# Router logits and the shared expert's first layer as one 264-column product with the tokens as weights

## The chip, the cores and the metric

The kernel runs on one core of one Trainium2 chip. The metric is device time in microseconds (us): the median of three runs, and, where a trace is read, the time of one profiled execution. All arithmetic on tensors is in float32, except for a few 0/1 matrices in bfloat16 in the routing.

## The reference, cut to what matters

The input is x of 2 sequences by 4096 positions by 512 features. A first part (test-time training) runs through the positions in order and keeps a state W for each sequence. A second part is a mixture of experts. Each is added to its input and layer-normalized.

```
x = layernorm(x + ttt(x))                  # W changes with every position
shared = silu(X @ sW1 + sb1) @ sW2 + sb2   # sW1: 512 x 256, sW2: 256 x 512
logits = X @ routing_W.T + expert_bias     # 8 experts: 8 columns
activation = sqrt(softplus(logits)); the 2 largest of 8 are kept as weights
routed = sum over the kept experts of weight * (silu(X @ rW1 + rb1) @ rW2 + rb2)
out = layernorm(x + shared + routed)
```

## The kernel before, in words

**Chunks and steps.** The positions are cut into 32 chunks of 128. A chunk holds 128 positions of both sequences, so 256 tokens (B = 2, T = 256). A loop over c = 0 to 31 makes one step for each chunk. In step c the following generators are interleaved.

- `step(c)` is the recurrence. It makes the residual R (matmuls `pr`), the output `po`, a triangular solve by three products (`pz` on TensorE, `Z` on VectorE), transposes of K (`pk`, copied to SBUF as the tile `K`), the solved product `pe` with `F` behind it, and the update of the state (`pw` on TensorE, `W` on VectorE, four times per sequence, and `pb` with `brep`).
- `prep(c + 1)` makes K and Q of the next chunk (`pkq`, copied by ScalarE) and their inner products (`pa`).
- `invert(c)` inverts small triangular blocks on VectorE (`X`), turns them through HBM (`dX`, `CT`) and makes `D` and `DT`, with which `pn` begins.
- `shared(c - 1)` is the mixture's first half for the chunk before. It finishes the normalization, transposes the tokens (`pt`, copied by ScalarE as `yT`), starts the routing (`router`: logits `pl` and `lg`, then `u`, Exp, `w`, Ln, ranks, `chosen`, Sqrt), computes the shared expert (`ph` and Silu into `h`, then `py`), and places the tokens by expert (`pq`, `place`, `row`, and scattered writes into tables in HBM).
- In steps 24 to 27 the routed expert tiles of chunks 0 to 22 run as well (`pg`, `phe`, `he`, `pye`). At the end of step 23, and again in step 31, `plan` turns the tables into lists of gathers (`codes`, `pc`, `gidx`). In steps 28 to 31 part of the results is collected (`acc` on VectorE). The rest follows behind step 31, with the routed tiles of chunks 23 to 30 and all experts for chunk 31.

**What sets the order.** `interleave` runs the generators so that each advances in proportion to a total given with it; the numbers after `yield` are the shares done. Chunk c's `shared` has the total SHARED = 15 (with 10 more for `plan`, and doubled in step 31). For TensorE and VectorE the order in which instructions are made this way is kept; each engine works through its own in order. ScalarE's order is the scheduler's.

**Buffers.** PSUM has three pools: `ps_p` with two buffers (`pkq`, `pa`, `pn`, `pz`), `ps_s` with three (`pr`, `po`, `pk`, `pe`, `pw`, `pb`) and `ps_f` with three (`pt`, `pl`, `ph`, `pq`, `py` and the routed tiles). The two `po` of a step keep two of `ps_s` until late, so that `pk`, `pe` and `pw` follow each other through the rest.

**Around the change.** The logits of a chunk are eight matmuls (2 sequences by 4 slices of 128 features) with a slice of `yT` as weights and 8 columns of `rw` moving through (line 480). The shared expert's first layer is eight matmuls with a 128 x 128 block of `w1` as weights and the 256 tokens moving through (line 594); its output has hidden units on the partitions, which is what `py` needs. Silu follows from PSUM with the bias per partition (line 597). The transposed K is copied from PSUM by ScalarE (line 439).

Of the kernel before, what the change touches and what calls it, by code (L numbers as in the profile page):

```python
# [40 lines left out]
F32 = mybir.dt.float32  # L41
# [3 lines left out]
ALU = mybir.AluOpType  # L45
AX = mybir.AxisListType

P = 128
# [53 lines left out]
def postln_block(ctx: ExitStack, tc: tile.TileContext, x, xT, thK, thV, thQ, w0, b0, masks, blk,  # L102
                 unit, order, rw, eb, w1s, b1s, w2s, b2s, b2e, wcat, out):
    nc = tc.nc
    B, S, D = x.shape
    NCH = S // P
    DC = D // P
    E = rw.shape[1]
    HF = w1s.shape[1]
    HC = HF // P  # L110
    T = B * P
# [6 lines left out]
    const = ctx.enter_context(tc.tile_pool(name="const", bufs=1))  # L118
# [6 lines left out]
    hp = ctx.enter_context(tc.tile_pool(name="hp", bufs=1))  # L125
# [3 lines left out]
    sm = ctx.enter_context(tc.tile_pool(name="sm", bufs=2))  # L129
# [4 lines left out]
    ps_f = ctx.enter_context(tc.tile_pool(name="ps_f", bufs=3, space=PSUM))  # L134
# [42 lines left out]
    load_x(0)  # L177
    load_x(1)

    rw_sb = const.tile([P, DC, E], F32, tag="rw", name="rw")  # L180
    nc.sync.dma_start(out=rw_sb, in_=rw.rearrange("(c p) e -> p c e", p=P))
    eb_sb = const.tile([P, E], F32, tag="eb", name="eb")
    nc.sync.dma_start(out=eb_sb, in_=eb.partition_broadcast(P))
    b1_sb = const.tile([P, HC], F32, tag="b1", name="b1")
# [2 lines left out]
    nc.sync.dma_start(out=b2_sb, in_=b2s.partition_broadcast(P))  # L187
    b1e_sb = const.tile([P, E, HC], F32, tag="b1e", name="b1e")
    nc.sync.dma_start(out=b1e_sb, in_=wcat[:, OB1:OB2].rearrange("(e p) h -> p e h", p=P))
    w1_sb = const.tile([P, DC, HF], F32, tag="w1", name="w1")  # L190
    nc.sync.dma_start(out=w1_sb, in_=w1s.rearrange("(c p) h -> p c h", p=P))
    w2_sb = const.tile([P, HC, D], F32, tag="w2", name="w2")
    nc.sync.dma_start(out=w2_sb, in_=w2s.rearrange("(c p) d -> p c d", p=P))

# [197 lines left out]
    def step(c):  # L392
# [25 lines left out]
        for s in range(B):  # L418

            ps = ps_s.tile([P, D], F32, tag="ps", name=f"po_{c}_{s}")  # L420
            for ec in range(DC):
                nc.tensor.matmul(ps, KQ[:, ec, s, 1, :], W[s][:, ec, :],  # L422
                                 start=(ec == 0), stop=False)
                if ec == 1:
                    if s == 0:
                        next(levels)
                    yield 2.0
            O.append(ps)
            if s == 0:
                next(levels)  # L430
            yield 2.0
            if s == 0:

                for r in range(B):
                    ps = ps_s.tile([P, DC, P], F32, tag="ps", name=f"pk_{c}_{r}")
                    for ec in range(DC):
                        nc.tensor.transpose(ps[:, ec, :], KQ[:, ec, r, 0, :], ident)
                    k = stepp.tile([P, DC, P], F32, tag="K", name=f"K_{c}_{r}")
                    nc.scalar.copy(k, ps)
                    K.append(k)  # L440
                    if r == 0:
                        Y = next(levels)
                    yield 1.5
# [26 lines left out]
        normed[c] = y, norm[1]  # L470


    def router(c, yT):
        def small(tag, shape=(P, B, E), bufs=1):
            return sm.tile(list(shape), F32, tag=tag, name=f"{tag}_{c}", bufs=bufs)

        ps = ps_f.tile([P, B, E], F32, tag="pf", name=f"pl_{c}")
        for s in range(B):
            for dc in range(DC):
                nc.tensor.matmul(ps[:, s, :], yT[:, dc, s, :], rw_sb[:, dc, :],  # L480
                                 start=(dc == 0), stop=(dc == DC - 1))
        lg = small("lg")
        nc.vector.tensor_tensor(lg, ps, eb_sb[:, None, :].broadcast_to([P, B, E]), ALU.add)


        u = small("u")
# [76 lines left out]
    def shared(c):  # L563

        gr = of_step.get(c)
        if gr and c == gr.c0:
            gr.begin()
        y, norm = normed.pop(c)
        next(norm)
        yield 1.5  # L570
        yT = ytp.tile([P, DC, B, P], F32, tag="yT", name=f"yT_{c}")
        for dc in range(0, DC, 2):
            ps = ps_f.tile([P, 2, B, P], F32, tag="pf", name=f"pt_{c}_{dc}")
            for s in range(B):
# [11 lines left out]
        yield 1.5  # L586
        for s in range(B):
            nc.gpsimd.tensor_tensor(y[:, s, :], y[:, s, :], b2_sb, ALU.add)
        ps = ps_f.tile([P, HC, T], F32, tag="pf", name=f"ph_{c}")
        h = hp.tile([P, HC, B, P], F32, tag="h", name=f"h_{c}")  # L590
        for hc in range(HC):
            cf = next(routing)
            for dc in range(DC):
                nc.tensor.matmul(ps[:, hc, :], w1_sb[:, dc, hc * P:(hc + 1) * P],
                                 yT[:, dc].rearrange("p s t -> p (s t)"),
                                 start=(dc == 0), stop=(dc == DC - 1))
            nc.scalar.activation(h[:, hc].rearrange("p s t -> p (s t)"), ps[:, hc, :],
                                 AF.Silu, bias=b1_sb[:, hc:hc + 1])
            yield 2.0
        next(routing, None)  # L600
        yield 1.0
        next(routing, None)
        if not gr:

            ps = ps_f.tile([E, B, P], F32, tag="pf", name=f"pct_{c}")
            for s in range(B):
                nc.tensor.transpose(ps[:, s, :], cf[:, s, :], ident)
            cfT = stepp.tile([E, B, P], F32, tag="K", name=f"cfT_{c}")
            nc.scalar.copy(cfT, ps)
            b2e_sb = stepp.tile([E, D], F32, tag="K", name="b2e")  # L610
            nc.sync.dma_start(out=b2e_sb, in_=b2e)
            yield 1.0
        for s in range(B):
            ps = ps_f.tile([P, D], F32, tag="pf", name=f"py_{c}_{s}")
            for hc in range(HC):
                nc.tensor.matmul(ps, h[:, hc, s, :], w2_sb[:, hc, :], start=(hc == 0),
                                 stop=(hc == HC - 1 and gr is not None))
            if not gr:
                nc.tensor.matmul(ps, cfT[:, s, :], b2e_sb, start=False, stop=True)
            nc.vector.tensor_tensor(y[:, s, :], ps, y[:, s, :], ALU.add)  # L620
            yield 2.0
        if not gr:
            last.extend((y, yT, cf))
            return
        nc.sync.dma_start(out=gr.base[rows].rearrange("(s p) d -> p s d", p=P), in_=y)
        if c == gr.c0 + gr.n - 1:
            yield from plan(gr)
# [350 lines left out]
```

## Time and the profile before

| What | Value |
|---|---|
| Time, median of three runs (lowest, highest) | 2758.53 us (2753.56, 2760.92) |
| Profiled execution: time, span of the trace | 2757.97 us, 2756.0 us |
| Busy share of the span: TensorE, VectorE, ScalarE, GpSimd | 96%, 47%, 27%, 28% |
| Granted TensorE clock, mean over the span | 0.989 |
| `ph`, line 594: instructions, mean of one | 512, 379 ns |
| `pl`, line 480: instructions, mean of one | 512, 251 ns |
| Transposes `pk`, line 437: instructions, mean of one | 256, 273 ns |
| Copy of K on ScalarE, line 439: instructions, mean of one | 64, 580 ns |

TensorE's instructions overlap, so the mean duration of one is longer than the time it takes from the engine. What it takes is read from the timeline, as the distance from one start to the next. A float32 matmul is recorded as two instructions, a float32 transpose as one; so 512 instructions of `pl` are 256 matmuls, eight for each of the 32 chunks. PEld is the loading of weights, which runs beside the matmuls. A line like "A <- B" in the waits says that an instruction writing A waited for one writing B.

### The profile page before, as it was taken

How to read it: one execution, taken by the hardware profiler on the slowest of the kernel's cores; microseconds unless marked ns; L12 is line 12 of the kernel's file. 1: busy time of each engine (PE TensorE's matmuls, PEld its weight loads, DVE VectorE, ACT ScalarE, POOL GpSimd, SP SyncE). 2: the span in 40 equal slices, each digit the busy share in tenths (PEclk: the TensorE clock that was granted, in tenths of full speed). 3: DMA queues.
4: the chain of work that ended last, by engine and by line, in shares of the span. 5: the costliest groups of instructions: out<-in, count | busy, mean ns of one | idle time of the engine just before them, and what ended most of it. 6: DMA issues, size and time to landing. Idle time of an engine off the chain costs nothing. (4 is left out here: it accounts for less than half of the span.)

```text
span 2756.0 us, 32318 instructions
## 1 busy us (share of the span) xinstructions
PE 2658.1 (96%) x10977; PEld 1718.3 (62%) x10977; DVE 1292.1 (47%) x4093; ACT 755.7 (27%) x1474; POOL 766.5 (28%) x767
## 2 busy tenths in 40 slices
PE   8999999999999999999999999999999999889887
PEld 6666666666666666666666676767667655546664
DVE  2455555444445555544445413223132388773238
ACT  1211122222221122222222322323223133334447
POOL 0121111111111111111112433243342355454445
PEclk9999999999999999999999999999999999999998
DMA  4122212111111211121112534344333467775666
GB/s 161 36 50 61 63 40 41 48 40 40 40 40 42 54 48 48 41 48 40 40 40 56 169 71 126 121 107 135 89 126 101 102 180 197 206 223 197 204 213 225
DMA packets 148787, 269.42 MB, mean 98 GB/s; under 512 B 61180, under 2 KB 62940, under 8 KB 145040
## 3 DMA queue, kind: packets, MB, share of 16 engines
q1 hardware_dynamic: 90608, 139.50, 17.5%
q0 software_dynamic: 49584, 111.61, 14.7%
q10 hardware_dynamic: 8432, 16.25, 1.7%
q8 instruction: 88, 1.44, 0.2%
q14 instruction: 75, 0.61, 0.1%
HBM read 333.37 MB, written 88.64 MB: 153 GB/s over the span
## 5 line engine op out<-in xcount | busy, mean ns | idle before, releaser
L347 DVE SCALAR_TENSOR_TENSOR X<-L,X 128x31 f32<-128x31 f32 (+22 forms) x1472 | 332.7, 274 | 27.5 <-DMA L<-dL 10.5
L557 POOL DMA_INDIRECT gt<-code,ri x124 | 123.7, 998 | 710.7 <-DVE ri L554 682.0
L790 PEld LDWEIGHTS phe<-gT,wb 128*128 128x128 f32 x2208 | 270.7, 194 | 75.4 <-issue 68.9
L804 DVE TENSOR_TENSOR o<-pye,wb 128x512 f32<-128x512 f32 x138 | 95.4, 691 | 452.1 <-PE pye L801 436.6
L790 PE MATMUL phe<-gT,wb 128*128 128x128 f32 x2208 | 273.7, 278 | 16.2 <-DMA wb<-wcat_in,widx 15.5
L801 PE MATMUL pye<-wb,he 128*128 128x512 f32 x552 | 266.8, 605 | 21.1 <-ACT he L794 20.4
L457 PE MATMUL pw<-F,K 128*128 128x512 f32 x512 | 244.6, 608 | 9.6 <-DVE W L458 8.1
L304 PE MATMUL pkq<-xT,thK 128*128 128x256 f32 x1024 | 242.9, 381 | 7.6 <-DMA thK<-thK_in 7.6
L304 PEld LDWEIGHTS pkq<-xT,thK 128*128 128x128 f32 x1024 | 195.3, 191 | 82.2 <-issue 61.6
L304 PE MATMUL pkq<-xT,thQ 128*128 128x256 f32 x1024 | 241.9, 380 | 2.6 <-ACT N L378 2.6
L422 PE MATMUL po<-W,kq 128*128 128x512 f32 x512 | 244.2, 600 | 0.0
L402 PE MATMUL pr<-thV,xT 128*128 128x512 f32 x512 | 241.8, 604 | 0.0
L407 PE MATMUL pr<-W,kq 128*128 128x512 f32 x512 | 240.1, 592 | 0.0
L772 POOL DMA_INDIRECT wb<-wcat_in,widx x138 | 141.9, 1028 | 342.9 <-DVE o L804 138.3
L304 PEld LDWEIGHTS pkq<-xT,thQ 128*128 128x128 f32 x1024 | 188.5, 191 | 40.9 <-issue 17.0
L311 ACT COPY kq<-pkq 128x256 f32<-128x256 f32 x256 | 83.2, 374 | 435.2 <-PE pkq L304 434.6
L794 ACT ACTIVATE he<-phe,wb 128x128 f32<-128x128 f32 x276 | 86.5, 363 | 419.1 <-PE phe L790 418.4
L458 DVE TENSOR_TENSOR W<-pw,W 128x512 f32<-128x512 f32 x256 | 173.4, 688 | 59.1 <-PE pw L457 56.6
L457 PEld LDWEIGHTS pw<-F,K 128*128 128x128 f32 x512 | 91.9, 191 | 141.3 <-issue 86.1
L766 POOL DMA_INDIRECT g<-gy,gidx x138 | 138.2, 1001 | 139.3 <-PE pg L781 115.0
L801 PEld LDWEIGHTS pye<-wb,he 128*128 128x128 f32 x552 | 98.6, 189 | 120.9 <-issue 76.7
L840 POOL DMA_INDIRECT z<-ge,sidx x124 | 136.5, 1101 | 100.8 <-DVE acc L857 33.9
(198 smaller groups left out, 3458.9 us busy)
## 6 DMA issues: line engine op xcount, KB each, us to landing
ge<-o SPq DMA_DIRECT2D x138, 256.0 KB, 2.0
xT<-xT_in SPq DMA_DIRECT2D x32, 512.0 KB, 3.7
x<-x_in SPq DMA_DIRECT2D x32, 512.0 KB, 3.7
L<-dL SPq DMA_DIRECT2D x128, 128.0 KB, 4.5
gy<-x SPq DMA_DIRECT2D x31, 512.0 KB, 2.8
gb<-x SPq DMA_DIRECT2D x31, 512.0 KB, 4.5
acc<-gb POOLq DMA_DIRECT2D x31, 512.0 KB, 5.2
y_out<-acc ACTq DMA_DIRECT2D x31, 512.0 KB, 6.0
```

The lines of the kernel that those rows point to most:

```text
L304: nc.tensor.matmul(ps[:, i].rearrange("p s t -> p (s t)"), th[:, dc, (ec + i) * P:(ec + i + 1) * P], xt[:, dc].rearrange("p s t -> p (s t) ...
L347: nc.vector.scalar_tensor_tensor(X[:, h, j + 1:], L[:, j + 1:, j], X[:, h, j:j + 1], X[:, h, j + 1:], ALU.mult, ALU.add)
L402: nc.tensor.matmul(ps, xt[:, dc, s, :], nthV_sb[:, dc, :], start=(dc == 0), stop=False)
L407: nc.tensor.matmul(ps, KQ[:, ec, s, 0, :], W[s][:, ec, :], start=False, stop=(ec == DC - 1))
L422: nc.tensor.matmul(ps, KQ[:, ec, s, 1, :], W[s][:, ec, :], start=(ec == 0), stop=False)
L457: nc.tensor.matmul(ps, K[s][:, ec, :], F[s], start=True, stop=True)
L458: nc.vector.tensor_tensor(W[s][:, ec, :], ps, W[s][:, ec, :], ALU.add)
L766: nc.gpsimd.indirect_dma_start(out=g_t[k], out_offset=None, in_=gr.y, in_offset=bass.IndirectOffsetOnAxis(ap=gr.gidx[:, k:k + 1], axis=0), ...
L772: nc.gpsimd.indirect_dma_start(out=wbuf[k % NW], out_offset=None, in_=wcat, in_offset=bass.IndirectOffsetOnAxis(ap=gr.widx[:, k:k + 1], ax ...
L790: nc.tensor.matmul(ps[:, hc, :], w[:, dc * HF + hc * P:dc * HF + (hc + 1) * P], t[:, dc, :], start=(dc == 0), stop=(dc == DC - 1))
L801: nc.tensor.matmul(ps, h[:, hc, :], w[:, O2 + hc * D:O2 + (hc + 1) * D], start=(hc == 0), stop=(hc == HC - 1))
L840: nc.gpsimd.indirect_dma_start(out=t, out_offset=None, in_=gr.ex, in_offset=bass.IndirectOffsetOnAxis(ap=gr.sidx[:, j, s, k:k + 1], axis=0 ...
```

## The change

The columns of the router are put beside those of the first layer in one tile, 264 columns wide. Per sequence, four matmuls with a slice of `yT` as weights give 128 tokens by 264 columns: 256 values of the first layer and 8 logits. ScalarE copies the 256 columns to SBUF (`pre`), VectorE adds the bias to the 8 logits. Four transposes (`pht`) turn `pre` back so that hidden units lie on the partitions, and Silu follows as before. The order of the parts of `shared` and its shares change with it, and SHARED goes from 15 to 13.5. Independently of this, VectorE instead of ScalarE copies the transposed K. The tiles `pre` and `h` have one tag with one buffer.

```diff
-    rw_sb = const.tile([P, DC, E], F32, tag="rw", name="rw")
-    nc.sync.dma_start(out=rw_sb, in_=rw.rearrange("(c p) e -> p c e", p=P))
...
-    w1_sb = const.tile([P, DC, HF], F32, tag="w1", name="w1")
-    nc.sync.dma_start(out=w1_sb, in_=w1s.rearrange("(c p) h -> p c h", p=P))
+    w1_sb = const.tile([P, DC, HF + E], F32, tag="w1", name="w1")
+    nc.sync.dma_start(out=w1_sb[:, :, 0:HF], in_=w1s.rearrange("(c p) h -> p c h", p=P))
+    nc.sync.dma_start(out=w1_sb[:, :, HF:], in_=rw.rearrange("(c p) e -> p c e", p=P))
...
-                    nc.scalar.copy(k, ps)
+                    nc.vector.tensor_copy(k, ps)
...
-    def router(c, yT):
+    def router(c, lg):
...
-        ps = ps_f.tile([P, B, E], F32, tag="pf", name=f"pl_{c}")
-        for s in range(B):
-            for dc in range(DC):
-                nc.tensor.matmul(ps[:, s, :], yT[:, dc, s, :], rw_sb[:, dc, :],
-                                 start=(dc == 0), stop=(dc == DC - 1))
-        lg = small("lg")
-        nc.vector.tensor_tensor(lg, ps, eb_sb[:, None, :].broadcast_to([P, B, E]), ALU.add)
...
-        yield 1.0
-        routing = router(c, yT)
+        yield 0.7
+
+        lg = sm.tile([P, B, E], F32, tag="lg", name=f"lg_{c}")
+        pre = hp.tile([P, B, HF], F32, tag="h", name=f"pre_{c}")
+        for s in range(B):
+            ps = ps_f.tile([P, HF + E], F32, tag="pf", name=f"ph_{c}_{s}")
+            for dc in range(DC):
+                nc.tensor.matmul(ps, yT[:, dc, s, :], w1_sb[:, dc, :],
+                                 start=(dc == 0), stop=(dc == DC - 1))
+            nc.scalar.copy(pre[:, s, :], ps[:, 0:HF])
+            nc.vector.tensor_tensor(lg[:, s, :], ps[:, HF:], eb_sb, ALU.add)
+            yield 1.5
+        routing = router(c, lg)
         next(routing)
-        yield 1.5
         for s in range(B):
             nc.gpsimd.tensor_tensor(y[:, s, :], y[:, s, :], b2_sb, ALU.add)
-        ps = ps_f.tile([P, HC, T], F32, tag="pf", name=f"ph_{c}")
+        yield 0.7
+        cf = next(routing)
+        ps = ps_f.tile([P, HC, T], F32, tag="pf", name=f"pht_{c}")
+        for hc in range(HC):
+            for s in range(B):
+                nc.tensor.transpose(ps[:, hc, s * P:(s + 1) * P],
+                                    pre[:, s, hc * P:(hc + 1) * P], ident)
         h = hp.tile([P, HC, B, P], F32, tag="h", name=f"h_{c}")
         for hc in range(HC):
-            cf = next(routing)
-            for dc in range(DC):
-                nc.tensor.matmul(ps[:, hc, :], w1_sb[:, dc, hc * P:(hc + 1) * P],
-                                 yT[:, dc].rearrange("p s t -> p (s t)"),
-                                 start=(dc == 0), stop=(dc == DC - 1))
             nc.scalar.activation(h[:, hc].rearrange("p s t -> p (s t)"), ps[:, hc, :],
                                  AF.Silu, bias=b1_sb[:, hc:hc + 1])
-            yield 2.0
+        yield 0.7
+        cf = next(routing)
+        yield 0.7
         next(routing, None)
-        yield 1.0
+        yield 0.5
         next(routing, None)
...
             nc.vector.tensor_tensor(y[:, s, :], ps, y[:, s, :], ALU.add)
-            yield 2.0
+            yield 3.0
...
-    TILE, COLLECT, SHARED, PLAN, DENSE = 4.5, 4.0, 15.0, 10.0, 64.0
+    TILE, COLLECT, SHARED, PLAN, DENSE = 4.5, 4.0, 13.5, 10.0, 64.0
```

Each `next(routing)` runs the router up to its next `yield`: the first makes `u` and Exp, the second `w`, Ln and the ranks, the third the rest of the activation with `chosen`, the fourth `pq`, the last `place` and the scattered writes.

More of the change, by code (lines that the diff above doesn't have):

```diff
@@ L569, in shared @@
         next(norm)
-        yield 1.5
+        yield 1.0
         yT = ytp.tile([P, DC, B, P], F32, tag="yT", name=f"yT_{c}")
@@ L582, in shared @@
             nc.sync.dma_start(out=gr.y[rows].rearrange("(s p) d -> p s d", p=P), in_=y)
-        yield 1.0
-        routing = router(c, yT)
+        yield 0.7
[10 more added lines that the diff above has]
+        routing = router(c, lg)
         next(routing)
-        yield 1.5
         for s in range(B):
             nc.gpsimd.tensor_tensor(y[:, s, :], y[:, s, :], b2_sb, ALU.add)
-        ps = ps_f.tile([P, HC, T], F32, tag="pf", name=f"ph_{c}")
+        yield 0.7
[5 more added lines that the diff above has]
+                                    pre[:, s, hc * P:(hc + 1) * P], ident)
         h = hp.tile([P, HC, B, P], F32, tag="h", name=f"h_{c}")
         for hc in range(HC):
-            cf = next(routing)
-            for dc in range(DC):
-                nc.tensor.matmul(ps[:, hc, :], w1_sb[:, dc, hc * P:(hc + 1) * P],
-                                 yT[:, dc].rearrange("p s t -> p (s t)"),
-                                 start=(dc == 0), stop=(dc == DC - 1))
             nc.scalar.activation(h[:, hc].rearrange("p s t -> p (s t)"), ps[:, hc, :],
                                  AF.Silu, bias=b1_sb[:, hc:hc + 1])
-            yield 2.0
+        yield 0.7
+        cf = next(routing)
+        yield 0.7
         next(routing, None)
-        yield 1.0
+        yield 0.5
         next(routing, None)
```

## The prediction

> **What bounds the kernel now.** I read the page first, then busy time by stretch, then the timelines of TensorE, ScalarE and VectorE over one ordinary step, and last the waits of steps 28 to 31. The page says who is nearly always busy:
>
> ```profile
> PE 2658.1 (96%) x10977; PEld 1718.3 (62%) x10977; DVE 1292.1 (47%) x4093; ACT 755.7 (27%) x1474; POOL 766.5 (28%) x767
> ```
>
> Busy time by stretch (columns: start:end, length, then busy time and instructions of TensorE, its weight loads, VectorE, ScalarE, GpSimd, then clock, DMA share, GB/s) shows where that holds:
>
> ```profile
> 500.00:1000.00 500.00, 500.00 (x1852) 311.43 (x1851) 250.82 (x847) 106.40 (x207) 79.92 (x80) 1.00 0.18 44
> ...
> 1800.00:2000.00 200.00, 193.66 (x988) 137.34 (x987) 54.74 (x151) 55.25 (x124) 74.70 (x75) 0.99 0.43 113
> ...
> 2200.00:2400.00 200.00, 186.28 (x682) 114.62 (x681) 164.56 (x505) 76.15 (x140) 103.29 (x99) 0.98 0.68 195
> ```
>
> Up to step 23 (100 to 1530 us) TensorE never rests; the list of its waits is empty between 100 and 1475 us. In steps 24 to 27 it rests for 2 to 3%. In steps 28 to 31 VectorE is busy for 82% and TensorE waits for it. So a cut in TensorE's work counts in full in the first part, and hardly in the last.
>
> What TensorE's work costs is the distance between starts, in its timeline (start, duration, line, operands):
>
> ```profile
> 1041.74 1.85 PE L480 MATMUL pl<-rw,yT 128*128 128x8 f32 x16
> 1043.44 3.68 PE L402 MATMUL pr<-thV,xT 128*128 128x512 f32 x8
> ...
> 1050.40 1.89 PE L594 MATMUL ph<-yT,w 128*128 128x256 f32 x8
> 1052.13 1.88 PE L407 MATMUL pr<-W,kq 128*128 128x512 f32 x4
> ...
> 1061.62 0.61 PE L384 MATMUL pz<-Z,N 128*128 128x128 f32 x4
> 1062.07 1.89 PE L594 MATMUL ph<-yT,w 128*128 128x256 f32 x8
> 1063.80 0.60 PE L437 MATMUL pk<-ident,kq 128*128 128x128 f32 x4
> 1064.23 0.61 PE L384 MATMUL pz<-Z,N 128*128 128x128 f32 x4
> ```
>
> `pl`: 16 instructions in 1.70 us, 106 ns each, though only 8 columns move. Four transposes take 0.43 us, 108 ns each. `ph`: 8 in 1.73 us, 216 ns each for 256 columns, 0.842 ns a column. So an 8-column instruction costs as much as a 128-column one: that is the price the change removes.
>
> **TensorE's sum.** Removed per chunk: `pl` 1.70 and `ph` 2 x 1.73 = 3.46, together 5.16 us. Added: 16 instructions of 264 columns at 222 ns = 3.56, and four transposes, 0.43; together 3.99. Saved: 1.17 us a chunk, 37 us for 32.
>
> [...]
>
> **The waits that come in steps 1 to 22.** I walk along the built order, counting from P, the end of the second `pz` (1062.07 in the fence). Before, `ph` stood behind it; now `pht` (0.43), `pk` (0.43), the third `pz` (0.45), `pkq` (1.72), the second `pk` (0.43), then half of `po` (1.72), `pq`. VectorE starts 0.2 us after a matmul's end (Z at 1062.27), and TensorE about 0.15 us after VectorE.
> - The third `pz` needs Z: 0.2 + 0.42 + 0.15 = 0.77; TensorE comes at 0.86. No wait, but the margin is 0.1.
> - The copy of K now queues on VectorE behind `w` and the ranks, which move here from the step's first half. `w` starts at 0.54, the ranks end 1.56 later (1045.62 to 1047.18), the copy starts at 2.0. The trace has no such copy on VectorE. Its bounds are ScalarE's 0.58 and VectorE's PSUM add of the same shape, 0.69; I take 0.69. Done and seen by TensorE at 2.9; `po` wants the buffer at 3.46. Hidden by `pkq`; uncovered, a VectorE 0.6 us later would cost each excess in full, with `po`, `pq`, `py` and `pe` queued behind.
> - `pq` needs `chosen`, which needs Ln, and ScalarE's order is now: Silu for the first half, Ln, Silu for the second, so one table load more. The rows:
>
> ```profile
> 1045.61 1.28 ACT L493 ACT_TABLE_LOAD   x1
> 1046.90 0.22 ACT L493 ACTIVATE lnw<-w 128x16 f32<-128x16 f32 x1
> ...
> 1064.00 0.47 ACT L597 ACTIVATE h<-ph,b 128x256 f32<-128x256 f32 x1 [3.24 <-PE ph L594]
> 1064.49 1.28 ACT L518 ACT_TABLE_LOAD   x1
> ```
>
>   `pht` ends at 0.43, Silu's load starts at 0.67, Silu at 1.97, Ln's load at 2.46, Ln at 3.75 to 3.97. The chain from `lnw` to `chosen` took 1.25 (1063.09 to 1064.34), so TensorE has it at 5.4 and comes at 5.18: a wait of 0.2 us. Bounds: 0 and 0.6.
>
> [...] The rows show no drain: a load starts 0.49 us after the start of a 0.47 us Silu, and its function 1.29 after it.
>
> Other edges have cover: `pre` (0.37 on ScalarE, by the 256-column copies of line 311) lies under 11.6 us of TensorE work before `pht`; `lg` holds up `X` by 0.45 us, so `D` comes at 23.7 us of the step and `pn` at 25.1; uncovered, that would cost 0.45. `py` now stands between the `pw`, and VectorE's add of it between the W updates: the two-buffer turn of `pw` costs 0.36 us as against 0.38. GpSimd's b2 adds and SyncE's write of the base come a few us later, with some 60 us before the next load needs that buffer. ScalarE loses 64 copies of 0.58 and gains 64 of 0.37 and some 20 table loads of 1.28, 12 us on an engine that is busy for 27%. The router's columns are loaded at the start by a transfer of the same size, some 90 us ahead of their use (first `pl` at 99.9 us). Cost of these: nothing.
>
> So a step saves 1.17 - 0.2 = 0.95 us; 22 steps: **-20.9** (bounds -25.7 and -12.5).
>
> **The other places.**
> - Steps 24 to 27: 4 x 1.17 = 4.7; a third is lost to waits for weights (10.5 us there before), since a faster TensorE only comes earlier: **-3.0** (-4.7 to -1).
> - Step 23: `ph` follows `pt` at once and waits 0.95 for `yT` (0.2 + 0.59 + 0.15); `pc` stands two `pw` later, so the first gathered tokens come 1.7 us later, where `pg` already waited 0.99. With the 1.17 saved: **+1.5** (0 to +3).
> - Steps 28 to 30: between `Z` and the last update of W, VectorE gets two copies (1.38), `w` and the ranks (1.6): 3.0 more, and it had 2.2 us free there. It ends 0.8 later; with gaps **+1.0 each, +3.0** (-3.5 if TensorE's saving stays, +9 if nothing is free).
> - Step 31 showed this:
>
> ```profile
> 2443.58 1.19 PE L376 MATMUL pn<-D,A 128*128 128x128 f32 x4 [5.74 <-DVE D L364]
> 2444.57 3.62 PE L422 MATMUL po<-W,kq 128*128 128x512 f32 x4
> ```
>
>   `D` waited behind `plan`'s chain; now it stands ahead of it, and that wait nearly goes. What is late next is `pc`: its gathers still follow the chain, 9 us long from the last list to the last landing, and `pk`, `po` and `pe` queue behind `pc`. I get 6 us there, and 3 at `pq`, for 3.5 to 5 won at `pn`: **+4.0** (-3 to +8). After the wait above, four `po` took 3.62 us where 1.88 is usual, so each long wait costs about 1.7 more.
> - Behind step 31: one chunk, partly under waits for ScalarE: **-0.5** (-1.2 to +1).
>
> Sum: -20.9 - 3.0 + 1.5 + 3.0 + 4.0 - 0.5 = **-15.9 us** on the profiled execution's 2757.97, so 2742.1. The median is 0.6 higher: 2742.6; I say **2742.5**.
>
> **The rivals.**
> - *The whole saving shows.* Every new wait falls into slack, as the K copy does: 2758.5 - 37 = 2721.5. For it: no wait before 1475 us. Against: VectorE's 82% in steps 28 to 30. 7%.
> - *Given back at the end.* Steps 28 to 30 lose 3 us each, step 31 loses 8, the tail 1, and `pq` waits 0.4 in the 22 steps, which then give 17: 2758.5 + 1.5 + 9 + 8 + 1 - 17 - 3 = 2759. Up to +-0.3% (8.3 us, about what a measurement can tell from no change): 16%.
> - *The chain through ScalarE decides, and it is slower.* Place: `pq` in steps 1 to 22, behind two table loads. If one more 1.28 us piece falls into the chain from `pht` to `chosen` (a later Exp, copies of K and Q ahead of Silu), each step waits 1.28 longer: 22 x 1.28 = 28 us, and -15.9 becomes +12, 2770.6. It decides from about 1.1 us a step for slower by 8.3. Against: these copies end 1.2 us before P. 9%.
> - *The logits' price was not the engine's.* If `pl` hid in gaps, nothing is saved. The rows before and after it are gapless, so I give this no share of its own.
>
> **How the numbers follow.** The forecast has 68%: from 2729 to 2750. The range reaches to the near half of the first rival and most of the second, and leaves out the third and the ends, under 2 in 10: 2727 to 2757. Faster by over 0.3%: 0.68 + 0.07 = 0.75; within: 0.16; slower: 0.09.
>
> **What would show it.** Right: `pl` gone, `ph` with 264 columns at 222 ns a start, steps of 61.8 us instead of 62.77 (1009.37 to 1072.14 from `pe` to `pe`), TensorE's new waits at `pq` for `chosen` of some tenths, a VectorE copy of K of about 0.69, about 20 table loads more than the 210 of before, longer steps 28 to 30. Wrong: a 264-column start far above 222 ns, waits of `pq` or `po` over 1 us in ordinary steps, or step 31 shorter than before.

## The result, and the profile after

The changed kernel takes 2755.11 us (median of 20 runs, 2749.30 to 2762.58), the kernel before 2760.31 us in the same comparison (20 runs, 2753.56 to 2766.44). The ratio is 0.9982, 95% interval 0.9973 to 0.9991: 5.2 us faster, where 15.9 were forecast. A second comparison on another chip (below) gave 3.6. The profiled execution took 2751.21 us, with a span of 2749.3.

The line of busy time, from the page of the changed kernel:

```profile
PE 2629.7 (96%) x10593; PEld 1683.8 (61%) x10593; DVE 1327.9 (48%) x4189; ACT 767.4 (28%) x1493; POOL 763.5 (28%) x767
```

TensorE has lost 28.4 us of work (2658.1 before) and the span only 6.7. So most of the saving came back as waiting. An ordinary step shows the saving itself. This is TensorE's timeline after (start, duration, line, operands):

```profile
1022.27 1.94 PE L582 MATMUL ph<-w,yT 128*128 128x264 f32 x8
1024.05 1.89 PE L304 MATMUL pkq<-xT,thK 128*128 128x256 f32 x8
...
1043.93 0.61 PE L384 MATMUL pz<-Z,N 128*128 128x128 f32 x4
1044.37 0.60 PE L596 MATMUL pht<-ident,pre 128*128 128x128 f32 x4
1044.81 0.60 PE L437 MATMUL pk<-ident,kq 128*128 128x128 f32 x4
...
1047.86 1.88 PE L422 MATMUL po<-W,kq 128*128 128x512 f32 x4
1049.70 0.19 PE L529 MATMUL pq<-chosen,before 128*128 128x8 bf16 x2
```

`ph` with 264 columns takes 1.78 us from start to start, 222 ns each; `pht` 0.44. Half of `po` takes 1.72, so `pq` could start at 1049.58 and starts at 1049.70. The list of TensorE's waits between 100 and 1475 us has one entry:

```profile
PE ph L582 <- ACT yT L570: 0.2, 1, 0.2
```

By place, each from one profiled execution (a step runs from its first `pr` to the next step's; "idle" is TensorE's idle time; "clock" is its busy time times one minus the granted clock, from stretches of 1 us):

| Place | Before, us | After, us | Difference | Forecast |
|---|---|---|---|---|
| start and step 0 | | | -0.9 | none |
| steps 1 to 22 | 1381.0 (62.77 each) | 1356.3 (61.64 each) | -24.7 | -20.9 |
| step 23 | 64.1 | 63.3 | -0.7 | +1.5 |
| steps 24 to 27 | 665.3 | 658.5 | -6.7 | -3.0 |
| steps 28 to 30 | 209.7 (idle 13.7, clock 4.6) | 217.2 (idle 22.5, clock 8.1) | +7.5 | +3.0 |
| step 31, to the first tile of the second group | 68.5 (idle 14.2, clock 5.7) | 79.1 (idle 22.1, clock 9.2) | +10.6 | +4.0 |
| from there to TensorE's end | 266.0 (idle 28.4, clock 4.4) | 273.3 (idle 34.2, clock 7.8) | +7.3 | -0.5 |
| behind TensorE's end | | | +1.0 | none |

The sum is -6.6; the spans give -6.7, the rest is rounding. So 33 us are won up to step 27 and 26 are lost behind. Of the loss, 10.4 us are a lower clock (3.5, 3.5 and 3.4).

Steps 28 to 30, waits of TensorE (us in total, times, longest), first before, then after:

```profile
PE pw L457 <- DVE W L458: 6.2, 6, 1.5
PE pb L463 <- DVE W L458: 3.4, 2, 2.6
PE pkq L304 <- ACT N L378: 2.6, 2, 2.0
PE pw L457 <- DVE x L453: 1.5, 3, 0.6
```

```profile
PE pkq L304 <- DVE Z L386: 9.8, 3, 3.3
PE pw L457 <- DVE x L453: 6.8, 3, 2.3
PE pb L463 <- DVE W L458: 6.0, 3, 3.1
```

There is one new wait of 3.2 us in each step, at `pkq` for `Z`, and a longer one for `x`. What `pkq` waits for is a buffer. `ps_p` has two. One holds the first half of Q until ScalarE has copied it; as long as it does, the other goes from `pz` to `pz`, and `pkq` can have it only when the third `Z` has read it. Step 28 before and then after, with ScalarE's copy of that half (`kq`), the second half's `pkq` and the third `Z`:

```profile
2230.33 0.35 ACT L311 COPY kq<-pkq 128x256 f32<-128x256 f32 x1
2230.92 0.37 ACT L311 COPY kq<-pkq 128x256 f32<-128x256 f32 x1 [0.24 <-issue]
...
2233.42 1.89 PE L304 MATMUL pkq<-xT,thQ 128*128 128x256 f32 x8
...
2234.70 0.42 DVE L386 TENSOR_TENSOR Z<-pz,DT 128x256 f32<-128x256 f32 x1
```

```profile
2202.00 0.41 DVE L386 TENSOR_TENSOR Z<-pz,DT 128x256 f32<-128x256 f32 x1
...
2202.47 2.45 PE L304 MATMUL pkq<-xT,thQ 128*128 128x256 f32 x8 [3.24 <-DVE Z L386]
...
2204.93 0.63 ACT L311 COPY kq<-pkq 128x256 f32<-128x256 f32 x2
```

Before, ScalarE copies 32.9 us into the step, and `pkq` starts ahead of the third `Z`. After, the copies stand behind Silu, Ln and Silu, 40.6 us into the step, and `pkq` waits for the third `Z`. That `Z` itself is hardly later: 37.6 us into the step, 37.2 before. The trace names only `Z`; that the buffers are the link follows from their number and these times.

Step 31 after, TensorE's waits in its timeline:

```profile
2399.20 0.21 PE L529 MATMUL pq<-chosen,before 128*128 128x8 bf16 x2 [3.01 <-DVE chosen L520]
...
2419.27 1.19 PE L376 MATMUL pn<-D,A 128*128 128x128 f32 x4 [6.45 <-DVE D L364]
...
2429.02 1.14 PE L384 MATMUL pz<-Z,N 128*128 128x128 f32 x4 [3.69 <-DVE Z L386]
...
2435.61 1.62 PE L759 MATMUL pc<-ident,codes 39*128 39x39 f32 x8 [3.71 <-DMA codes<-gt,r]
```

The wait of `pn` for `D` has not gone. What such a wait costs on top shows in the busy time by stretch (start:end, length, TensorE's busy time, then the others; the third number from the right is the granted clock):

```profile
2412.00:2414.00 2.00, 0.82 (x2) 0.00 (x0) 0.00 (x0) 0.00 (x0) 0.00 (x0) 1.00 0.44 66
2414.00:2416.00 2.00, 0.00 (x0) 0.00 (x0) 0.00 (x0) 0.00 (x0) 0.00 (x0) 0.87 0.88 367
2416.00:2418.00 2.00, 0.00 (x0) 0.00 (x0) 0.00 (x0) 0.00 (x0) 0.00 (x0) 0.50 1.03 395
2418.00:2420.00 2.00, 0.73 (x3) 0.76 (x4) 1.47 (x7) 0.00 (x0) 0.00 (x0) 0.50 0.26 98
2420.00:2422.00 2.00, 2.00 (x6) 0.97 (x5) 1.86 (x7) 1.50 (x3) 0.97 (x1) 0.50 0.04 8
```

TensorE stops at about 2412.8, the clock is 0.50 from about 2415.5, and the work that comes at 2419.3 still runs at 0.50 until 2422.3.

### The profile page after: what moved, and what is told of

Its sections match the earlier page's. It is cut to its first block, busy times and chain, and to the rows that moved or that the text cites. A ratio compares the mean times of both kernels' runs of the same rounds, so it can differ in the third digit from the quotient of the medians.

```text
span 2749.3 us, 31544 instructions
## 1 busy us (share of the span) xinstructions
PE 2629.7 (96%) x10593; PEld 1683.8 (61%) x10593; DVE 1327.9 (48%) x4189; ACT 767.4 (28%) x1493; POOL 763.5 (28%) x767
## 4 chain that ended last, share of the span: by engine, by line
PE 85%; DMA 4%; issue 4%; DVE 4%; ACT 2%; POOL 1%; SPq 0%; POOLq 0%; DVEq 0%; ACTq 0%
PE pkq L304 16%; PE pye L806 8%; PE pr L402 8%; PE pr L407 8%; PE po L422 8%; PE phe L795 7%; PE pw L457 7%; PE ph L582 4%; PE py L621 4%; PE pa L317 3%; PE pb L463 2%; PE pg L786 2%; PE po L452 2%; PE pe L446 2%; PE pz L384 1%
## 5 line engine op out<-in xcount | busy, mean ns | idle before, releaser
L806 PE MATMUL pye<-wb,he 128*128 128x512 f32 x552 | 269.8, 612 | 28.6 <-ACT he L799 20.5
L795 PE MATMUL phe<-gT,wb 128*128 128x128 f32 x2208 | 273.6, 278 | 11.9 <-DMA wb<-wcat_in,widx 10.4
L407 PE MATMUL pr<-W,kq 128*128 128x512 f32 x512 | 231.9, 592 | 0.0
```

The costliest lines, as they stand in the source:

```text
L407: nc.tensor.matmul(ps, KQ[:, ec, s, 0, :], W[s][:, ec, :], start=False, stop=(ec == DC - 1))
L795: nc.tensor.matmul(ps[:, hc, :], w[:, dc * HF + hc * P:dc * HF + (hc + 1) * P], t[:, dc, :], start=(dc == 0), stop=(dc == DC - 1))
L806: nc.tensor.matmul(ps, h[:, hc, :], w[:, O2 + hc * D:O2 + (hc + 1) * D], start=(hc == 0), stop=(hc == HC - 1))
```

## The experiments

In each comparison the kernel before ran on the same chip; its median went from 2743.8 to 2761.8 us over the chips. So times are given as differences of medians from the kernel before of the same comparison, with the ratio on record and its interval; that ratio is not the quotient of the two medians. Place lengths are from one profiled execution each.

These ran side by side on one chip: `pl` twice, both experiments on K and "new form up to step 27 only"; the three "old form" kernels and "`plan` ahead of `C`"; "the changed kernel again", "ranks and Ln earlier", the same with `plan` first, and "new form with ranks early to step 27"; the four with `ph` together or built on it; the two with the placing behind `py`. The changed kernel itself ran only in the first comparison and in the third of these groups. Across groups, differences from the kernel before are not comparable to better than about 10 us (an estimate: two kernels below, 32.1 and 44.5 us faster on two chips, differ by 2.5 us in their traces up to step 22).

Theory A was that TensorE's saving is real up to step 27 and is lost behind, place by place, by the new order of the routing on VectorE, ScalarE and GpSimd. Its rivals: the copies of K alone make the loss (B), step 31 inherits its loss (C), the end is set by transfers or is scatter (D). The others are named where they come up.

The mixed kernels hold both forms of `shared` and `router`; the old router reads its 8 columns from the joint tile. Their edit is

```diff
+    half = lambda c: shared(c) if NEW(c) else shared_old(c)
...
-            parts.append((amount * (2 if c == NCH - 1 else 1), shared(c - 1)))
+            parts.append((amount * (2 if c == NCH - 1 else 1), half(c - 1)))
```

with SHARED 13.5 or 15 as the form needs.

### Are the prices right?

**`pl` done twice** (kernel before):

```diff
+        for twice in range(2):
             for s in range(B):
                 for dc in range(DC):
                     nc.tensor.matmul(ps[:, s, :], yT[:, dc, s, :], rw_sb[:, dc, :], ...
```

> The kernel before with each `pl` product done twice, 16 matmuls of 8 columns in place of 8 per chunk; the second overwrites the first with the same values. If a matmul of 8 columns takes 106 ns from TensorE, an ordinary step grows by 1.70 us: 23 x 1.7 = 39, and 2 to 4 us more in steps 24 to 27: 2800 us (2795 to 2808). [...]

Measured: +103.9 us (ratio 1.038, 1.0362 to 1.0397), where 41 to 43 were expected. Nine of the 22 ordinary steps take 64.56 us, which is 1.79 more: 112 ns for each added instruction, so the price of 106 ns stands. The other steps take 66.24 (4) or 67.9 (9), 1.68 or 3.36 more again, with no wait. TensorE's timeline of one of them, and the clock:

```profile
163.81 4.47 PE L481 MATMUL pl<-rw,yT 128*128 128x8 f32 x32
168.14 6.20 PE L402 MATMUL pr<-thV,xT 128*128 128x512 f32 x8
```

```profile
165.00:166.00 1.00, 1.00 (x11) 1.00 (x11) 0.57 (x5) 0.00 (x0) 0.00 (x0) 1.00 0.00 0
166.00:167.00 1.00, 1.00 (x8) 1.00 (x8) 0.00 (x0) 0.00 (x0) 0.00 (x0) 0.69 0.16 28
167.00:168.00 1.00, 1.00 (x7) 1.00 (x6) 0.00 (x0) 0.00 (x0) 0.00 (x0) 0.50 0.04 5
```

The clock halves although TensorE is busy without a gap; `pr` takes 6.20 us where 3.60 is usual. In steps 1 to 22 this costs 37.6 us, which with 22 x 1.7 gives 75 of the 76 us that these steps grew by.

**K on ScalarE again** (changed kernel):

```diff
-                    nc.vector.tensor_copy(k, ps)
+                    nc.scalar.copy(k, ps)
```

> The changed kernel with one part undone: K is copied by ScalarE again, in all steps. Theory A (the new routing order puts the copy behind table loads): from the end of `pht`, ScalarE has Silu's load, Silu, Ln's load, Ln, Silu's load, the second Silu (to about 5.75 us), and only then the copy of K (0.58), while `po` wants the buffer at 3.46. So TensorE waits some 2.9 us for K in each of steps 1 to 22, 64 us, and as much in other steps: 2820 us (2800 to 2850), with waits of `po` for K in ordinary steps. Theory B (the copies on VectorE are what the end lost, and ordinary steps do not need them there): ordinary steps stay at 61.6 us, steps 28 to 31 give 5 to 15 us back: 2740 to 2750 us.

Measured: +65.8 us (1.024, 1.0223 to 1.0257); theory A. TensorE's waits between 100 and 1475 us:

```profile
PE po L422 <- ACT K L439: 55.7, 21, 2.9
```

That is 2.65 at a time, close to the 2.9 worked out from ScalarE's queue. Steps 1 to 22 take 72.1 us longer than in the changed kernel; 10.6 of them are a lower clock. So the two halves of the change are not independent. Once Ln stands between the two Silu, the copy of K must leave ScalarE.

**K on VectorE** (kernel before, the opposite line):

> The kernel before with one part of the change alone: K is copied by VectorE. Theory A (the end is lost by the routing's new place more than by the copies): ordinary steps stay at 62.8 us, since the copy has cover there; steps 28 to 30 lose about 1.0 us each and step 31 about 1, so 2764 us (2760 to 2769). Theory B (the copies alone make the loss at the end): steps 28 to 31 lose the 18 us that they lost with the whole change: 2778 us (2772 to 2786).

Measured: +6.0 us (1.003, 1.0013 to 1.0046), the size that theory A gave. But its place lengths (steps 28 to 30 208.2, step 31 65.9) are not longer than before's, so its trace does not show where the 6 us are; that execution took 2747.35 us, 5.4 less than this kernel's median. Theory B falls: with the change these four steps lose 18 us, and the copies alone lose nothing of that size.

### Where is it lost?

**New form up to step 27 only** (`NEW = c <= 26`, K on VectorE for steps up to 27):

> The new product, its order and the copy of K by VectorE for chunks 0 to 26, so up to step 27; from step 28 on the old `pl`, the old `ph`, the old order of the routing and K on ScalarE. Theory A (savings and losses belong to their places and add): 32 us are won up to step 27 and nothing is lost behind: 2728 us (2722 to 2735), with a step 31 of 68 us to the first tile of the second group and a lead of some 30 us that stays to the end. Theory D (the end is set by transfers or by something that an earlier arrival cannot move): the lead of 32 us at step 28 melts in the tail to under 15 us: 2745 to 2758 us.

Measured: -32.1 us (0.9892, 0.9874 to 0.9910), steps of 61.64, step 31 67.1. Savings and losses belong to their places and add; the end keeps a lead.

**Old form in step 31 only** (`NEW = c != 30`):

> The changed kernel with the old form (`pl`, old `ph`, old order of the routing, K on ScalarE) for chunk 30 alone, which is worked in step 31. Theory A (step 31 loses by its own new order): step 31 goes from 79.1 to about 68 us (start to the first tile of the second group), the rest stays: 10 to 11 us faster than the changed kernel, 13 to 16 us faster than before. Theory C (the loss of step 31 is carried in by steps 28 to 30): step 31 stays at 75 us or more, and the time is that of the changed kernel, 3 to 6 us faster than before.

Measured: -12.1 us (0.9960, 0.9947 to 0.9972), a little less than the 13 to 16 expected; step 31 66.1, steps 28 to 30 still 216.1. So step 31's loss is its own, and theory C falls.

**Old form in steps 28 to 30 only** (`NEW = c not in (27, 28, 29)`):

> The changed kernel with the old form and K on ScalarE in steps 28 to 30 alone. Theory A (VectorE is the bound there, and the copies of K and the ranks add 3 us a step between two updates of W): steps 28 to 30 take 204 to 210 us in place of 217, so 7 to 12 us faster than the changed kernel, 11 to 17 us faster than before. Theory C (these steps are late for what step 27 leaves over, the first group's collection): they stay at 215 us or more and nothing is won.

Measured: -3.1 us (0.9989, 0.9979 to 0.9999). Steps 28 to 30 take 208.3, as theory A says, and step 31 81.5; but 11 to 17 were expected, and the time is not better than the changed kernel's -5.2 and -3.6. These two were measured on other chips, though. Within this chip the places do explain the times: the kernel with the old form in step 31 is 8.9 us faster by its median, and in the traces this one is 7.8 us shorter in steps 28 to 30, 15.4 longer in step 31 and 1.6 longer behind it. If the new form's lengths on this chip are put into each of its four kernels, the changed kernel would take 2746 to 2750 us here (an estimate), 2 to 6 us more than the kernel before.

**Old form behind step 31 only** (`NEW = c != 31`):

> The changed kernel with the old form for chunk 31 alone, which runs behind step 31 beside the routed tiles of the second group. Theory A (the stretch behind step 31 loses because the chunk's parts stand otherwise among the tiles): from the first tile to the end 264 to 266 us, 273 with the change: 8 us faster than the changed kernel, 12 to 14 us faster than before. Theory D (that stretch ends when its transfers end, and an earlier or later start is made up there): under 3 us from the changed kernel.

Measured: -0.5 us (0.9995, 0.9984 to 1.0006), where theory A had 12 to 14. In the trace the stretch takes 267.5 us, in the other three kernels of this chip 269.8 to 273.5. Since the changed kernel did not run there, -0.5 does not tell whether this won anything.

**The changed kernel again:**

> The changed kernel itself once more, for its place lengths on a second chip and beside the next three. If the lengths belong to the order of the instructions: steps 28 to 30 214 to 220 us, step 31 77 to 82, from the first tile of the second group to the end 270 to 275, and 0 to 8 us faster than before. If they are scatter of one execution: one of them moves to the length of before (210, 68, 266).

Measured: -3.6 us (0.9985, 0.9975 to 0.9995); 215.2, 81.7 and 272.8 us. These lengths belong to the order of instructions, not to one execution. Steps 24 to 27 are less steady: 653.0 to 659.0 us in the eight traces with the same form there.

### Step 31: one number

**`plan` ahead of `C`** (changed kernel):

```diff
-            yield 3.0
+            yield 2.0 if c == NCH - 2 else 3.0
```

> The changed kernel with one number changed: in step 31 alone the shares behind the two `py` are 2.0 again, not 3.0, so that `plan`'s chain stands ahead of `C` and `D` on VectorE, as it did before, and not behind. Theory A (in step 31 VectorE stands idle 7 us for `CT`, and `plan`'s 6.7 us chain, ready by then, is queued behind it, so `pc` is late by as much): `plan` runs in that gap, `pc` waits under 1 us, and step 31 goes from 79.1 to 70 to 73 us: 6 to 9 us faster than the changed kernel. Theory E (step 31 is late for Ln's and Sqrt's place behind four table loads, and for the clock after it, whatever the order of `plan`): step 31 stays at 77 us or more.

Measured: -11.3 us (0.9955, 0.9941 to 0.9969); step 31 takes 67.8 us. VectorE's timeline in the changed kernel, then here (`C`, and first and last of `plan`'s chain, lines 693 and 749):

```profile
2418.42 0.24 DVE L360 STREAM_TRANSPOSE C<-CT 128x64 f32<-128x64 f32 x1 [7.23 <-DMA CT<-dX]
...
2420.68 0.16 DVE L693 TENSOR_TENSOR count<-next,first 128x8 f32<-128x8 f32 x1
...
2427.18 0.19 DVE L749 TENSOR_TENSOR sidx<-sl,row 128x32 int32<-128x32 f32 x1
```

```profile
2409.27 0.15 DVE L693 TENSOR_TENSOR count<-next,first 128x8 f32<-128x8 f32 x1
...
2415.78 0.19 DVE L749 TENSOR_TENSOR sidx<-sl,row 128x32 int32<-128x32 f32 x1
...
2417.73 0.24 DVE L360 STREAM_TRANSPOSE C<-CT 128x64 f32<-128x64 f32 x1 [0.75 <-DMA CT<-dX]
```

`C` starts 36.9 us into the step with the change and 36.3 here: it waits for `CT`, whatever stands beside it. What differs is that the chain now runs inside that wait. (SyncE issues the load of `CT` 31.6 us into the step with the change and 26.1 us in the kernel before.) The waits at `pz` (3.69) and `pc` (3.71) are gone; `pn` still waits 5.59, `pq` still 3.01. Idle time falls from 22.1 to 13.6, the clock's share from 9.2 to 6.3.

### Steps 28 to 30: two waits, one behind the other

**Ranks and Ln earlier** (changed kernel):

```diff
             nc.vector.tensor_tensor(lg[:, s, :], ps[:, HF:], eb_sb, ALU.add)
+            if s == B - 1:
+                routing = router(c, lg)
+                next(routing)
             yield 1.5
-        routing = router(c, lg)
-        next(routing)
+        cf = next(routing)
         ... (additions of b2)
         yield 0.7
-        cf = next(routing)
```

> The changed kernel with the routing's first two parts one share earlier: `u` and Exp directly behind the second `lg`, and `w`, Ln and the ranks ahead of the GpSimd additions, one share before `pht`. On VectorE the ranks then stand between the first and the second `Z`, and on ScalarE Ln stands ahead of both Silu, so that Silu is loaded once a step. Theory A (the end is lost because the ranks stand between the last `Z` and the updates of W, and because Ln parts the two Silu): steps 28 to 30 go from 217 to 208 to 213, `pq` in step 31 waits under 1.5 us in place of 3.0, the stretch behind step 31 takes 265 to 270 in place of 273; step 31 keeps its loss behind `plan`: 8 to 18 us faster than the changed kernel. Theory B (the copies of K, or the place of `py`, make the loss): steps 28 to 31 keep their lengths, and the time is within 4 us of the changed kernel's.

Measured: -12.8 us (0.9949, 0.9934 to 0.9964). Ordinary steps take 61.53 us, 0.11 less, so that was the wait at `pq`. Step 31 takes 77.6, behind it 270.7. `pq` in step 31 still waits 3.0. Most of the gain stands where none was expected: steps 24 to 27 take 650.9 us, and 659.0 in the changed kernel on the same chip; why was not tried. But steps 28 to 30 stay at 218.8, not 208 to 213. TensorE's waits there:

```profile
PE pb L463 <- DVE W L458: 16.1, 3, 7.7
PE pw L457 <- DVE x L453: 7.0, 3, 2.4
PE pz L384 <- DVE Z L386: 2.2, 3, 0.7
```

The 9.8 us for `Z` at `pkq` are gone, and `pb` waits 16.1 where it waited 6.0. The same three instructions in step 28:

```profile
2186.43 0.65 ACT L311 COPY kq<-pkq 128x256 f32<-128x256 f32 x2 [0.97 <-PE pkq L304]
...
2190.70 1.89 PE L304 MATMUL pkq<-xT,thQ 128*128 128x256 f32 x8
...
2192.34 0.41 DVE L386 TENSOR_TENSOR Z<-pz,DT 128x256 f32<-128x256 f32 x1
```

The third `Z` is not earlier (37.3 us into the step, 37.6 in the changed kernel), although the ranks no longer stand ahead of it. ScalarE's copy is: 31.4 us in place of 40.6, since Ln stands ahead of both Silu. So `pkq` has a free buffer. By these times it is Ln's place on ScalarE, and not that of the ranks on VectorE, that made this wait; the two were not moved apart. GpSimd's timeline in step 28, and what VectorE waits for behind it:

```profile
2201.00 1.00 POOL L846 DMA_INDIRECT z<-ge,sidx  x1 [0.30 <-DVE ri L546]
2202.30 1.03 POOL L549 DMA_INDIRECT gt<-code,ri  x1 [0.30 <-DVE fst L276]
...
2206.24 0.98 POOL L549 DMA_INDIRECT gt<-code,ri  x1 [0.30 <-issue]
...
2213.68 1.00 POOL L846 DMA_INDIRECT z<-ge,sidx  x1 [0.30 <-DVE W L458]
```

```profile
2219.09 0.75 DVE L863 SCALAR_TENSOR_TENSOR acc<-z,cw,acc 128x512 f32<-128x512 f32 x1 [4.39 <-DMA z<-ge,sidx]
```

Four scattered writes stand ahead of five gathers, each about 1.3 us from the next. VectorE waits 4.4 us for a gather, with the last updates of W queued behind that sum.

**Both halves of `ph` together** (changed kernel; VectorE's list showed 9.6 us of waiting at `lg`):

```diff
-            yield 1.5
+        yield 3.0
```

> The changed kernel with both halves of `ph` made together, where the first stood; the share between them is added behind the second. Theory L (in steps 28 to 30 VectorE, in order, stands some 3.2 us a step at the second `lg` for the second half of `ph`, and the sums of the collection queued behind it slide into the updates of W): steps 28 to 30 take 207 to 212 us in place of 215 to 219, the idle time at `lg` falls from 9.6 us to under 2, ordinary steps stay at 61.6: 6 to 10 us faster than the changed kernel, 9 to 15 us faster than before. Theory G (VectorE has more work there, whatever the order): steps 28 to 30 stay at 215 us or more, and the time within 3 us of the changed kernel's.

Measured: +1.4 us (0.9999, 0.9988 to 1.0010); steps 28 to 30 take 225.3. Theory L falls: the steps got longer. The wait at `lg` went, and VectorE waits 12.7 us for `CT` instead.

**Placing behind `py`, ranks early, `plan` first:**

```diff
+        late = 26 < c < NCH - 2
+        if not late:
-        next(routing, None)
+            next(routing, None)
...
+        if late:
+            next(routing, None)
         nc.sync.dma_start(out=gr.base[rows]...
```

> The kernel with the earlier ranks and `plan` first, and in steps 28 to 30 the placing (`place` to `gt`) behind the second `py`, so that on GpSimd's queue the gathers `z` go ahead of the four `gt`. Theory Q (each wait hides the other: first the third `Z` behind the ranks, then the `z` behind `gt`): with both away steps 28 to 30 take 205 to 212 us in place of 219, TensorE's waits for W at `pb` fall from 16 us to under 5, step 31 stays at 67 to 70: 30 to 38 us faster than before. Theory T (the collection's transfers set these steps, wherever the writes stand): 215 us or more, 20 to 27 us faster than before.

Measured: -30.7 us (0.9889, 0.9873 to 0.9904). Steps 28 to 30 take 203.5 us, the shortest of all traces (203.6 to 209.7 with the old form there); idle 14.4, clock 1.7. TensorE's waits there:

```profile
PE pw L457 <- DVE x L453: 6.8, 3, 2.3
PE pb L463 <- issue: 2.4, 1, 2.4
PE pb L463 <- DVE W L458: 2.0, 2, 1.4
```

**Placing behind `py` alone** (ranks as the change put them):

> The changed kernel with the placing behind the second `py` in steps 28 to 30 alone; the ranks stay where the change put them. Theory Q: the wait of 3.2 us for the third `Z` stays in each step, and behind it VectorE is late by as much: steps 28 to 30 take 212 to 217 us, 4 to 9 us faster than before. If `gt` alone makes the loss: 205 to 210, 10 to 15 us faster than before.

Measured: 214.3 us for steps 28 to 30, as theory Q says, but -0.9 us for the whole (0.9998, 0.9988 to 1.0008), where 4 to 9 were expected; step 31 took 85.0 here. Neither move alone shortens the three steps by more than 3 us; both together take off 12 to 14 (from 215.2 and 217.2 in the two traces of the changed kernel). Each wait hid the other.

### Do the repairs add?

| Kernel | Difference, us (ratio, interval) | Steps 28 to 30 | Step 31 | From there on |
|---|---|---|---|---|
| ranks early, `plan` first | -25.5 (0.9905, 0.9887 to 0.9923) | 218.9 | 69.0 | 272.2 |
| the same, `ph` together | -20.3 (0.9926, 0.9913 to 0.9939) | 222.1 | 66.8 | 273.7 |
| the same, old form behind step 31 | -17.1 (0.9931, 0.9918 to 0.9944) | 226.3 | 70.3 | 273.7 |
| new form with ranks early to step 27, then old | -44.5 (0.9832, 0.9815 to 0.9850) | 209.4 | 67.7 | 268.7 |
| the same, `ph` together | -38.1 (0.9855, 0.9839 to 0.9871) | 208.0 | 66.9 | 273.6 |

The edits are those above, combined. In the order of the table:

> The kernel with the earlier ranks, and with `plan` ahead of `C` in step 31 as well (shares of 2.0 behind the two `py` there). Theory A: both gains add; step 31 takes 66 to 70 us, and the whole is 22 to 32 us faster than before, nearly all that the first 27 steps win. Theory F (one wait is hidden behind the other, so that only the larger counts): 12 to 18 us faster than before.

> The changed kernel with three moves: the halves of `ph` together, the ranks and Ln one share earlier, `plan` ahead of `C` in step 31. All parts of the new form are kept in all steps. If the three losses are separate: ordinary steps 61.5, steps 28 to 30 207 to 212, step 31 66 to 70, behind it 270 to 273: 32 to 42 us faster than before. If they hide each other: 20 to 28.

> The same with the old form for chunk 31, behind step 31. If that stretch loses by the order of the chunk's parts among the tiles: 264 to 268 us there and 4 to 7 us faster than with the new form. If it ends by its transfers: within 2 us of it.

> The new form with the earlier ranks for chunks 0 to 26 (K on VectorE up to step 27), the old form from step 28 on. Theory A: as the mixed kernel before it, 32 us faster than before, and another 0.1 us in each of steps 1 to 22 where `pq` waited: 32 to 36 us faster than before, with ordinary steps of 61.5 to 61.6 us. If VectorE's wait for Exp ahead of `w` delays the second `Z`: ordinary steps over 61.8 us and under 28 us won.

> The new form with the halves together and the earlier ranks for chunks 0 to 26, the old form from step 28 on. Nothing in steps 1 to 27 waited at `lg`, so the gain is that of the kernel with the halves apart: 33 to 46 us faster than before, ordinary steps of 61.5 us.

On one chip the changed kernel is 3.6 us faster than the one before, 12.8 with the ranks early and 25.5 with `plan` first as well. So `plan` brings 12.7 on top of the ranks, and neither hides the other. With the halves of `ph` together it is 20.3, less than the 32 to 42 expected; steps 28 to 30 are not shorter by that move. The old form behind step 31 won nothing beside the kernel without it (17.1 and 20.3, on one chip). "New form with ranks early to step 27, then old" was expected at 32 to 36, as without the early ranks; at 44.5 it is better than that, but the 32.1 is from another chip, and no trace shows the difference. The best version keeps the new form where TensorE is the bound and the old one behind it: 2712.57 us against 2757.05, better than both kernels.

## Why the prediction was right or wrong

**Right: the price and the saving.** `pl` cost 106 ns an instruction (112 when doubled), `ph` 222 ns a start. Steps 1 to 22 gave 24.7 us, inside the bounds named; the 0.2 us at `pq` were 0.1. Both prices that the prediction read from rows held in the runs: 106 ns for an 8-column instruction (+1.79 us a step for 16 more of them), and 1.28 us for each of the two table loads in the chain to `pq` (still 1.28, and no step from 1 to 22 in which `pq` waits for more than 0.12).

Step 23 and steps 24 to 27 were 2.2 and 3.7 us better than forecast. In the second the reason failed: the waits for weights, which were to eat a third of the saving, fell from 10.5 us to 4.1 (5.4 in the second trace of the changed kernel).

**Wrong: steps 28 to 30 (+3.0 forecast, +7.5).** The term was made from VectorE's amount of work: "3.0 more, and it had 2.2 us free there". VectorE's work in these steps hardly grew; it is busy for 175.7 us after and 172.3 before. The step that failed is another: what the new order gives ScalarE was summed up as "Cost of these: nothing". With Ln between the two Silu, the copies of Q's first half went from 32.9 to 40.6 us into the step, `pkq` had to take the buffer of the third `Z`, and TensorE waits 3.2 us there in each step. The prediction looked at what `pz`, `po` and `pq` wait for, and not at this edge; its third rival names copies of Q in ScalarE's queue and drops them, because in ordinary steps they end ahead of P. Behind this wait lay a second one (the gathers behind `gt`), which comes out only when the first is away. The square of four kernels shows both: 217.2, 218.8, 214.3, 203.5.

**Wrong: step 31 (+4.0 forecast, +10.6).** The failing step is "now it stands ahead of it, and that wait nearly goes". `D` did stand ahead of `plan`, but it waited for `CT`: 6.45 us at `pn` in place of 5.74, not 3.5 to 5 won. And `plan`, ready and 6.7 us long, queued behind the wait. So 3.69 at `pz` and 3.71 at `pc` came on top of the 3.0 at `pq`, which was forecast; `pt`, which the term leaves out, waited 3.2 us less than before. With `plan` before `C` step 31 takes 67.8 us (68.5 before the change); that is shown. Why `CT` came 14.3 us after the end of `X` was not tried.

**Wrong: the clock.** The prediction noted that four `po` took 3.62 us after a long wait and put 1.7 on each, but only in step 31. The lower clock is 10.4 of the 26 us lost, in all three places.

**Wrong, and open: behind step 31 (-0.5 forecast, +7.3).** In the traces that stretch takes 263 to 274 us with the old form and 270 to 274 with the new one. The one pair that differs in this alone on one chip has 273.7 with either form, and the old one won nothing in the median. So it is not shown that the new form loses there. The traces of the first pair show more waiting at `pye` (21.5 us in place of 16.6, the longest for `he`, 6.07 in place of 1.9) and for `wb` (6.3 in place of 5.0, up to 3.24); no run tells what causes it.

**The rivals.** The one that came closest is the second, given back at the end, with 16%: it had 9 us lost in steps 28 to 30 and 8 in step 31, and 7.5 and 10.6 were measured. But it had 0.4 us at `pq` in each ordinary step (0.1 came) and 1 us behind step 31 (7.3 came). Its sum is given as 2759; its terms give 2758. The stated range held the 2755.11 us only because it reached over most of this rival; the forecast's own stretch, 2729 to 2750, did not hold it. The third did not come: no ordinary step waits for the chain through ScalarE by more than 0.12 us. But the run with K on ScalarE shows how near it was: one more piece in that queue cost 2.65 us at a time.

## What to carry to other kernels

When the order on an engine changes, ask also which buffers it now gives free later. Here an engine that is busy for a third of the time copied one tile 7.7 us later, and that became a wait of 3.2 us for TensorE in each of three steps, at an instruction that needs no result of it. When an instruction is moved ahead of a chain, ask when its own input lands; if it waits, all that is ready stands behind it, as `plan`'s 6.7 us did behind a wait of 7.23. Where one bottleneck gives way to another, use the new form only in the stretch whose bound it relieves: here the changed kernel's 3.6 us became 44.5 on the same chip.

## What the runs showed of the hardware that was not expected

- Most long waits of TensorE were followed by a clock of 0.50, so that the work behind them was slow too: four `pn` behind the wait of 6.45 us took 1.19 us, and 0.61 in an ordinary step. Between 100 and 2725 us of the changed kernel TensorE stops eleven times for more than 3 us. After ten of these stops the clock is at 0.50, from 2.2 to 4.8 us after the stop on and for 3.41 or 6.83 us; after one, of 3.24 us in step 29, it stayed at 1.00. Three stops of 2.0 to 2.3 us were followed by it too. In all, the lower clock is 10.4 us more than before in the changed kernel's last part.
- In the kernel with `pl` twice the clock fell without any idle time before it. While 32 instructions of `pl` with 8 columns ran back to back (3.4 us at full clock), it went to 0.50 in 13 of 22 steps, 2.4 to 3.4 us after the first of them and for 3.41 us (4 steps) or 6.83 us (9 steps). The steps grew by half of that, 1.68 or 3.36 us. With 16 of them (1.7 us), in the kernel before, it stayed at 1.00 in these steps.
